# Layer 1's second convolution as a two-phase filter along the columns: five plane products in place of six, its input's sum on VectorE in two parts

## The chip, the cores and the metric

The kernel runs on one core of a Trainium2 chip. The metric is the device time of one execution in microseconds (us); lower is better. TensorE (PE) multiplies matrices, VectorE (DVE) and ScalarE (ACT) work on elements, GpSimd (POOL) works on elements and issues DMAs, SyncE (SP) issues DMAs.

## The reference, cut to what matters

x has 16 images of 16 channels of 256 x 256 in fp32. Layer 0 is a Fourier-type layer that the change doesn't touch. Layer 1 computes, with H = 128:

```
f     = mish(conv2d(each channel alone, W1 (4,1,3,3)))        # 4 features for each channel
top, bot = f[:, :, :128], f[:, :, 128:]
ker   = Wspan * relu(Wred . bot)                              # 9 taps for each position
top_inv = sum over the 3x3 taps of patches(top) * ker         # "involution"
shuffled = rows of top_inv, then of bot rolled by one channel # 64 planes of 256 x 256
out   = mish(conv2d(shuffled, W2 (16,64,3,3)) + b2)           # the second convolution
gate  = sigmoid(3-tap filter over channels of mean(out))
result = x * gate (added to the layer's input)
```

Of `out` only the mean of each channel over all positions is used.

## The kernel before, in words

Layer 0 takes the first 3,500 us or so. Layer 1 (function `layer1`) cuts each image b into nine units, s = 0 to 8: eight full ones and a smaller tail unit. A unit runs through

- `lower` (L1042): first convolution of the lower half, two groups of matmuls through `conv1` (L1029) into the two-buffer PSUM pool `ps1`, four Mish activations on ACT (L1048, `bot`);
- `reduce` (L1050): `pr` matmuls with 32 output columns (L1056), two Relu (L1065, `r`);
- `upper(0)` and `upper(1)` (L1068): first convolution of the upper half, each one group in `ps1` (L1029) and eight Mish activations of 32 partitions (L1077, `wide`); the tail unit has `upper(0)` alone;
- `spread` (L1084): eight copies on POOL (L1089, L1090);
- `involution(0)` to `involution(3)` (L1092): each two groups of a `pd` matmul (L1097) and three VectorE operations (L1105, L1108), then stores of the result to `cf` in DRAM by POOL's DMAs (L1119 to L1131); `bot` is stored too (L1149).

The second convolution works an image later. `conv2_rows` (L1154) loads `rows`, 17 pairs of image rows with 64 planes each, into one of two SBUF buffers `rows2`. In a partition, `rows` holds per pair 258 values: a zero, the 128 odd columns, the 128 even columns, a zero. So the even columns and the odd columns are two planes, and one 3-tap filter along the columns is three products of a shifted plane with a weight. `conv2(b, s, acc)` (L1159) is a generator with two parts, q = 0 for the odd output columns and q = 1 for the even ones. Each part makes three plane products (dx) times two blocks of rows (blk) times four 32-column tiles of PE (j) into one PSUM tile `c2ps`, and a Mish on ACT (L1182) whose accumulator adds up the output. The pool `ps2` of `c2ps` has one buffer. An fp32 matmul leaves two records in the trace: a product is 8 matmuls of the program, 16 records; a part has 48 records.

PE, ACT, DVE and POOL run in the order in which the program is written (a manual schedule); each engine goes through its own list in order and waits at semaphores. DMAs on SP are placed by a scheduler. In step i, with `now` unit i, `nxt` unit i + 1 and `second` the convolution of the image before, the order is (L1256 to L1295):

```
begin_unit(i + 2); conv2_rows for the next step; second = conv2(b - 1, s, acc)
nxt.lower(); now.involution(0); next(second)     # part q = 0
nxt.reduce(); now.involution(1); nxt.upper(0); now.involution(2)
nxt.upper(1); nxt.spread(); next(second)         # part q = 1
now.involution(3)
```

`begin_unit` loads `z` by SP for two units ahead. In the steps with s = 8 there is no convolution; `gate` (L1185) starts there, in front of `nxt.lower()`: it adds up `acc` on VectorE (`total`, `totals`), multiplies on PE (`pg`, L1205), takes an Exp on ACT, and in the steps that follow scales the image on POOL (L1221) and stores it (L1230). After the last image, eight steps hold the convolution alone: this is called the tail.

Of the kernel before, what the change touches and what calls it, by code (L numbers as in the profile page):

```python
# [10 lines left out]
F32 = mybir.dt.float32  # L11
I32 = mybir.dt.int32
AF = mybir.ActivationFunctionType
ALU = mybir.AluOpType
# [7 lines left out]
P = 128  # L22
# [34 lines left out]
def load(nc, pool, src, shape, name):  # L57
    t = pool.tile(shape, F32, tag=name, name=name)
    nc.sync.dma_start(out=t, in_=src)
    return t  # L60
# [872 lines left out]
def layer1(ctx, tc, d, zn, cf, mr, nb):  # L933
# [7 lines left out]
    nc = tc.nc  # L941
    H = N // 2
    wp = ctx.enter_context(tc.tile_pool(name="l1w", bufs=1))
    zp = ctx.enter_context(tc.tile_pool(name="l1z", bufs=4))
    fp = ctx.enter_context(tc.tile_pool(name="l1f", bufs=2))
    rp = ctx.enter_context(tc.tile_pool(name="l1r", bufs=3))
# [3 lines left out]
    psd = ctx.enter_context(tc.tile_pool(name="psd", bufs=3, space=PSUM))  # L950
    ps2 = ctx.enter_context(tc.tile_pool(name="ps2", bufs=1, space=PSUM))
# [6 lines left out]
    wr = load(nc, wp, d["wr"], [P, 32], "wr")  # L958
    dw = load(nc, wp, d["dw"], [P, P], "dw")
    dwt = load(nc, wp, d["dwt"], [P, P], "dwt")  # L960
    c2 = load(nc, wp, d["c2"], [P, 2, 3, 32], "c2")
    pm = load(nc, wp, d["pm"], [P, 3, C], "pm")
    weca = wp.tile([P, 3], F32, name="weca")
    nc.sync.dma_start(out=weca, in_=d["weca"].to_broadcast([P, 3]))
# [8 lines left out]
    b2 = load(nc, wp, d["b2"], [P, 1], "b2")  # L973
# [20 lines left out]
    for t in rows2:  # L994
        for x in (0, N + 1):
            nc.gpsimd.memset(t[:, :, x : x + 1], 0.0)

    def load_rows(b, half, j, h):

        z = zp.tile([P, 8, N + 2], F32, tag="z", name="z")  # L1000
        flat = z.rearrange("p c x -> p (c x)")
        row = C * (N + 2)
        if j < 4:

            m = 8 * (N + 2) - 2
            src = zn[b, H * half + 30 * j, 8 * h, 0:1]
            for dx in range(3):
                win = bass.AP(src.tensor, src.offset + dx, [[row, 32], [1, m]])
                nc.sync.dma_start(out=flat[32 * dx : 32 * dx + 32, :m], in_=win)
            for i in range(2):  # L1010
                win = bass.AP(src.tensor, src.offset + (32 + i) * row, [[1, 3], [1, m]])
                nc.sync.dma_start(out=flat[96 + 3 * i : 99 + 3 * i, :m], in_=win)
            return z
        m = 4 * (N + 2) - 2
        src = zn[b, H * half + 120, 0, 0:1]
        for dx in range(3):
            for c in range(4):
                p = 40 * dx + 10 * c
                win = bass.AP(src.tensor, src.offset + dx + 4 * (N + 2) * c, [[row, 10], [1, m]])
                nc.sync.dma_start(out=flat[p : p + 10, :m], in_=win)  # L1020
        return z
# [132 lines left out]
    def conv2_rows(b, s):  # L1154
        t = rows2[(8 * b + s) % 2]
        flat = cf[b % 4].rearrange("(t y) f c x -> (y f c) t x", y=2)
        nc.sync.dma_start(out=t[:, :, 1 : N + 1], in_=flat[:, 16 * s : 16 * s + 17])

    def conv2(b, s, acc):  # L1159


        t = rows2[(8 * b + s) % 2]

        begin = ((H + 1, 1, H + 2), (0, H + 1, 1))
        for q in range(2):

            pool, tag = (psd, "d") if q and b == nb - 1 else (ps2, "c2")
            ps = pool.tile([P, 4, H], F32, tag=tag, name="c2ps")
            for blk in range(2):
                for dx in range(3):  # L1170
                    x = begin[q][dx]
                    for j in range(4):
                        nc.tensor.matmul(  # L1173
                            ps[32 * j : 32 * j + 32],
                            lhsT=c2[:, blk, dx, :],
                            rhs=t[:, 4 * j + blk : 4 * j + blk + 4, x : x + H],
                            start=(blk, dx) == (0, 0),
                            stop=(blk, dx) == (1, 2),
                        )
            e = rp.tile([P, 4, H], F32, tag="e2", name="e2", bufs=2)  # L1180
            k = 2 * s + q
            nc.scalar.activation(e, ps, AF.Mish, bias=b2, accum_out=acc[:, k : k + 1])  # L1182
            yield

    def gate(b, acc):  # L1185

# [53 lines left out]
    def begin_unit(i):  # L1240
        if i < len(order):
            b, s = order[i]
            units[i] = Unit(b, i, *blocks[s])

    E = mybir.EngineType
    with tc.manual_schedule(engines={E.PE, E.Activation, E.DVE, E.Pool}):
        begin_unit(0)
        begin_unit(1)
        u = units[0]
        u.lower()  # L1250
        u.reduce()
        u.upper(0)
        u.upper(1)
        u.spread()
        acc, last = None, iter(())
        for i in range(9 * nb + 12):  # L1256
            b, s = divmod(i, 9)
            now, nxt = units.pop(i, None), units.get(i + 1)
            begin_unit(i + 2)
            second = iter(())  # L1260
            if s == 8 and b < nb:
                conv2_rows(b, 0)
            if s == 8 and b and b <= nb:
                last = gate(b - 1, acc)
                next(last)
            if s < 8 and b and b <= nb:
                if s == 0:
                    acc = sm.tile([P, 16], F32, tag="acc", name="acc")
                if s < 7:
                    conv2_rows(b - 1, s + 1)  # L1270
                second = conv2(b - 1, s, acc)
            if nxt:
                nxt.lower()
            if now:
                now.involution(0)
            next(second, None)
            if nxt:
                nxt.reduce()
            if s == 8:
                next(last, None)  # L1280
            if now:
                now.involution(1)
            if nxt:
                nxt.upper(0)
            if now:
                now.involution(2)
            if s == 8:
                next(last, None)
            if nxt:
                nxt.upper(1)  # L1290
                nxt.spread()
            next(last, None)
            next(second, None)
            if now:
                now.involution(3)  # L1295
# [159 lines left out]
@with_exitstack  # L1455
def forward(ctx, tc, d):
    nb = d["x"].shape[0]
    dram = ctx.enter_context(tc.tile_pool(name="dram", bufs=1, space=DRAM))
    keep = ctx.enter_context(tc.tile_pool(name="keep", bufs=1))
    al = dram.tile([NF, 2, 64, nb, N], F32, name="al")  # L1460
    bd = dram.tile([nb, P, P], F32, name="bd")
    hd = dram.tile([2, 2, 64, nb, C, N], F32, name="hd")
    tabs = (
        dram.tile([P, 2, C, N], F32, name="td"),
        dram.tile([NF, P, 384], F32, name="avd"),
        dram.tile([P, 2, C, N], F32, name="ed"),
    )
    zn = dram.tile([nb, N + 2, C, N + 2], F32, name="zn")
    cf = dram.tile([4, N + 2, 4, C, N], F32, name="cf")
    mr = keep.tile([P, nb, G, 2], F32, name="mr")  # L1470
    layer0_forward(tc, d, al, bd, tabs)
    layer0_mix(tc, d, al, hd, tabs)
    layer0_back(tc, d, hd, bd, zn, mr, tabs[2])
    layer1(tc, d, zn, cf, mr, nb)
# [25 lines left out]
```

## Time and profile before

| what | value |
|---|---|
| three runs, median (lowest to highest) | 7309.22 us (7302.86 to 7325.03) |
| the profiled execution: its own time, its span | 7312.28 us, 7310.5 us |
| mean granted PE clock | 0.969 |
| busy share of the span: PE, DVE, ACT, POOL | 92%, 68%, 52%, 47% |
| L1173, PE, the second convolution | 12288 records, 1391.9 us busy |
| L1182, ACT, its Mish | 256 of 687 ns |
| L1077, ACT, Mish of `upper` | 2176 of 680 ns |
| L1108, L1105, DVE, involution | 2176 of 691 ns, 1088 of 684 ns |

The time is that of one execution; the span is from the first to the last instruction of the profile, and the rest lies around it. Busy shares are averages over stages with different limits: a share below 100% doesn't say that an engine has room in every stage. PE's records overlap: the duration of one is longer than its distance to the next.

### The profile page before, as it was taken

Reading aid. Unit: us, or ns where it says so; the run is one execution under the profiler, and the core shown is the slowest. Engines: PE = TensorE matmul, PEld = TensorE weight load, DVE = VectorE, ACT = ScalarE, POOL = GpSimd, SP = SyncE. Lnnn points to the kernel's source line nnn. Section 1 sums busy time; section 2 is a strip of 40 time slices with the busy share of each in tenths; the row PEclk is TensorE's granted clock in tenths of the full one; section 3 lists DMA queues with packets and bytes.
Section 4 is the critical chain, followed back from the end, with each engine's and each line's share of the span. In section 5 each row is a group of like instructions: output and inputs, shape, how many; then the busy total and the mean of one; then the engine's idle time right before and its main releaser. Section 6 shows DMA issues by size and latency. Waiting matters only on the chain.

```text
span 7310.5 us, 147410 instructions
## 1 busy us (share of the span) xinstructions
PE 6750.3 (92%) x57640; PEld 3787.1 (52%) x57640; DVE 4970.2 (68%) x9465; ACT 3811.4 (52%) x5915; POOL 3470.0 (47%) x4612
## 2 busy tenths in 40 slices
PE   7889999899999998999789999999999999999997
PEld 5777778666667776777433333333333333333332
DVE  8999975466666665888666666666666666666662
ACT  2223333466666665222366666666666666666662
POOL 2334445322222222666554666556665555655663
PEclk9889999999999999999899999999999999999998
DMA  3344444433333333999767888888888888888886
GB/s 100 112 115 125 119 125 125 124 100 97 96 94 98 99 99 107 321 327 326 227 195 218 249 256 257 249 259 248 267 260 243 253 248 268 253 247 254 252 267 219
DMA packets 716089, 1443.59 MB, mean 197 GB/s; under 512 B 98954, under 2 KB 525254, under 8 KB 673638
## 3 DMA queue, kind: packets, MB, share of 16 engines
q1 hardware_dynamic: 567206, 959.76, 43.8%
q0 software_dynamic: 148192, 474.40, 20.9%
q8 instruction: 460, 7.54, 0.4%
q14 instruction: 231, 1.89, 0.1%
HBM read 877.12 MB, written 556.47 MB: 196 GB/s over the span
## 4 chain that ended last, share of the span: by engine, by line
PE 71%; DVE 16%; DMA 4%; ACT 4%; issue 3%; POOL 1%; SPq 0%; DVEq 0%; ACTq 0%; POOLq 0%
PE c2ps L1173 18%; PE c L1029 12%; PE pd L1097 12%; PE ph L700 5%; PE ps L643 5%; PE pg L665 4%; PE px L313 3%; ACT wide L1077 3%; DVE alb L607 2%; PE pu L207 2%; PE pr L1056 2%; PE py L860 2%; PE pv L214 2%; PE py L861 2%; DVE u L224 2%
## 5 line engine op out<-in xcount | busy, mean ns | idle before, releaser
L1077 ACT ACTIVATE wide<-c,b 32x512 f32<-32x512 f32 x2176 | 1479.3, 680 | 354.2 <-PE c L1029 302.6
L1105 DVE TENSOR_TENSOR t<-pd,r 64x512 f32<-64x512 f32 x1088 | 744.3, 684 | 1287.8 <-PE pd L1097 1262.3
L1108 DVE TENSOR_TENSOR top<-pd,t 32x512 f32<-32x512 f32 x2176 | 1504.1, 691 | 53.7 <-DMA cf<-bot 1.2
L1173 PE MATMUL c2ps<-rows,c 128*32 128x512 f32 x12288 | 1391.9, 600 | 16.4 <-DMA rows<-cf 16.4
L1089 POOL COPY wide<-wide 32x1031 f32<-32x1031 f32 (+1 forms) x576 | 569.6, 989 | 1236.2 <-ACT wide L1077 1208.7
L1029 PE MATMUL c<-z,w 102*128 102x512 f32 x2048 | 1014.5, 628 | 139.2 <-ACT wide L1077 116.6
L1097 PE MATMUL pd<-wide,dw 128*128 128x512 f32 x2048 | 1013.1, 617 | 6.0 <-ACT r L1065 2.9
L1173 PEld LDWEIGHTS c2ps<-rows,c 128*32 128x32 f32 x12288 | 400.3, 109 | 972.0 <-issue 891.6
L720 POOL DMA_DIRECT2D hd<-h x512 | 324.3, 640 | 1198.7 <-DVE h L713 1174.1
L1029 PEld LDWEIGHTS c<-z,w 102*128 102x128 f32 x2048 | 401.5, 198 | 676.5 <-issue 486.9
L1097 PEld LDWEIGHTS pd<-wide,dw 128*128 128x128 f32 x2048 | 377.1, 194 | 613.6 <-issue 447.5
L1182 ACT ACTIVATE e<-c2ps,b 128x512 f32<-128x512 f32 x256 | 176.0, 687 | 831.1 <-PE c2ps L1173 828.4
L1090 POOL COPY wide<-wide 32x1031 f32<-32x1031 f32 (+1 forms) x576 | 573.0, 995 | 36.1
L700 PE MATMUL ph<-ix,yt 64*128 64x256 f32 x4128 | 502.3, 390 | 7.2 <-issue 6.6
L643 PE MATMUL ps<-tt,lt 128*64 128x256 f32 x4224 | 495.5, 384 | 12.6 <-DMA tt<-td 10.0
L313 PE MATMUL px<-wxn,u 128*64 128x256 f32 x4224 | 481.9, 379 | 8.0 <-ACT o L320 7.9
L207 PE MATMUL pu<-fy,eo 128*128 128x128 f32 x2048 | 426.8, 292 | 26.8 <-DVE u L224 21.8
L700 PEld LDWEIGHTS ph<-ix,yt 64*128 64x128 f32 x4128 | 393.1, 190 | 94.0 <-issue 46.8
L1048 ACT ACTIVATE bot<-c,b 128x512 f32<-128x512 f32 x544 | 344.3, 684 | 175.2 <-PE c L1029 167.9
L873 POOL TENSOR_TENSOR x<-x,o 128x512 f32<-128x512 f32 x256 | 324.4, 1267 | 216.6 <-DVE o L872 198.5
L607 DVE TENSOR_SCALAR alb<-alc,m 128x1024 f32<-128x1024 f32 x330 | 419.9, 1396 | 0.0
L214 PE MATMUL pv<-at,eo 128*128 128x128 f32 x2048 | 413.3, 285 | 0.0
(204 smaller groups left out, 10418.6 us busy)
## 6 DMA issues: line engine op xcount, KB each, us to landing
rows<-cf SPq DMA_DIRECT2D x128, 2176.0 KB
z<-zn SPq DMA_DIRECT2D x768, 257.8 KB
cf<-top POOLq DMA_DIRECT2D x512, 240.0 KB, 7.0
cf<-bot POOLq DMA_DIRECT2D x96, 840.0 KB, 11.6
alc<-al SPq DMA_DIRECT2D x264, 256.0 KB
zn<-zb SPq DMA_DIRECT2D x128, 516.0 KB
o<-zn SPq DMA_DIRECT2D x128, 516.0 KB
z<-in_x SPq DMA_DIRECT2D x64, 1024.0 KB
```

Of the source, the lines that this page charges most:

```text
L207: nc.tensor.matmul(pu[:, xh, e].rearrange("p v m -> p (v m)"), lhsT=lhs, rhs=fy[:, e], start=True, stop=True,)
L313: nc.tensor.matmul(ps[64 * k : 64 * k + 64, :, h], lhsT=u[:, h, part, g0 + j + k].rearrange("p f c -> p (f c)"), rhs=wxn[:, h, part], star ...
L643: nc.tensor.matmul(ps[64 * h : 64 * h + 64, v], lhsT=lt[:, h, k, 1 - v : 3 - v].rearrange("p l f c -> p (l f c)"), rhs=tt[:, h, k], start= ...
L700: nc.tensor.matmul(ph[q][:, e], lhsT=yt[lanes, i].rearrange("p t k -> p (t k)"), rhs=ix[lanes, i], start=n == 0, stop=n == 3,)
L1029: nc.tensor.matmul(ps[:, a], lhsT=w, rhs=z[:k, c : c + 2, 0:N], start=True, stop=True)
L1077: nc.scalar.activation(self.feat[64 - 32 * q : 96 - 32 * q, f, self.groups[g], :H], ps[q][32 * f : 32 * f + 32], AF.Mish, bias=b1[0][32 * ...
L1089: nc.gpsimd.tensor_copy(flat[0:32, f, 1:m], flat[64:96, f, 0 : m - 1])
L1090: nc.gpsimd.tensor_copy(flat[96:128, f, 0 : m - 1], flat[32:64, f, 1:m])
L1097: nc.tensor.matmul(ps, lhsT=dwt if self.tail else dw, rhs=self.feat[:, f, cs, :H], start=True, stop=True,)
L1105: nc.vector.tensor_tensor(t[64:128], ps[:64], self.r[:, cs], ALU.mult)
L1108: nc.vector.tensor_tensor(self.top[32 * f : 32 * f + 32, cs, q], ps[lanes], t[lanes], ALU.add)
L1173: nc.tensor.matmul(ps[32 * j : 32 * j + 32], lhsT=c2[:, blk, dx, :], rhs=t[:, 4 * j + blk : 4 * j + blk + 4, x : x + H], start=(blk, dx) = ...
```

## The change

With the odd column plane O, the even column plane E and the weights w0, w1, w2 of the three taps, the kernel before computes even(k) = w0 O(k-1) + w1 E(k) + w2 O(k) and odd(k) = w0 E(k) + w1 O(k) + w2 E(k+1): six products. The changed kernel computes A(k) = w1 E(k) (one product, copied from PSUM to SBUF by ACT into `mid`), even(k) = A(k) + w0 O(k-1) + w2 O(k) (two products), pair(k) = E(k) + O(k-1) (a sum on VectorE of two SBUF inputs, rows 0 to 8 and then rows 9 to 16), and odd(k) = w0 pair(k) + (w1 + w2) pair(k+1) - [w0 O(k-1) + w2 O(k) + A(k+1)] (two products and a subtraction). The weights w1 + w2 are added up once (`c2s`). VectorE takes `even`, `both` and `odd` out of PSUM; the Mishes read SBUF. `conv2` now has four parts, placed at other points of the step: A after `involution(0)`, the two products of `even` after `involution(1)`, those of `odd` in front of `involution(3)`, and the Mish of `odd` after the next step's `lower`. `conv2_rows` stands in front of `lower` as before, and `gate` now starts after `lower`. In the last image the products of `even` take a buffer of the pool `psd`, as part q = 1 did.

```diff
+    c2s = wp.tile([P, 2, 32], F32, name="c2s")
+    nc.vector.tensor_tensor(c2s, c2[:, :, 1], c2[:, :, 2], ALU.add)
...
+    pair = wp.tile([P, 17, H + 1], F32, name="pair")
+    mid = [wp.tile([P, 4, H + 1], F32, name=f"mid{i}") for i in range(2)]
+    for t in mid:
+        nc.gpsimd.memset(t[:, :, H : H + 1], 0.0)
...
     def conv2(b, s, acc):
         t = rows2[(8 * b + s) % 2]
-        begin = ((H + 1, 1, H + 2), (0, H + 1, 1))
-        for q in range(2):
-            pool, tag = (psd, "d") if q and b == nb - 1 else (ps2, "c2")
+        def sums(lo, hi):
+            nc.vector.tensor_tensor(
+                pair[:, lo:hi], t[:, lo:hi, H + 1 :], t[:, lo:hi, : H + 1], ALU.add
+            )
+
+        def products(terms, n=0):
+            pool, tag = (psd, "d") if n % 2 and b == nb - 1 else (ps2, "c2")
             ps = pool.tile([P, 4, H], F32, tag=tag, name="c2ps")
-            for blk in range(2):
-                for dx in range(3):
-                    x = begin[q][dx]
+            for i, (w, src, x) in enumerate(terms):
+                for blk in range(2):
                     for j in range(4):
                         nc.tensor.matmul(
                             ps[32 * j : 32 * j + 32],
-                            lhsT=c2[:, blk, dx, :],
-                            rhs=t[:, 4 * j + blk : 4 * j + blk + 4, x : x + H],
-                            start=(blk, dx) == (0, 0),
-                            stop=(blk, dx) == (1, 2),
+                            lhsT=w[:, blk],
+                            rhs=src[:, 4 * j + blk : 4 * j + blk + 4, x : x + H],
+                            start=(i, blk) == (0, 0),
+                            stop=(i, blk) == (len(terms) - 1, 1),
                         )
-            e = rp.tile([P, 4, H], F32, tag="e2", name="e2", bufs=2)
+            return ps
+
+        def pooled(y, q):
             k = 2 * s + q
-            nc.scalar.activation(e, ps, AF.Mish, bias=b2, accum_out=acc[:, k : k + 1])
-            yield
+            nc.scalar.activation(y, y, AF.Mish, bias=b2, accum_out=acc[:, k : k + 1])
+
+        a = mid[s % 2]
+        nc.scalar.copy(a[:, :, :H], products([(c2[:, :, 1], t, H + 1)]))
+        sums(0, 9)
+        yield
+        ps = products([(c2[:, :, 0], t, 0), (c2[:, :, 2], t, 1)], 1)
+        even = rp.tile([P, 4, H], F32, tag="even", name="even", bufs=2)
+        nc.vector.tensor_tensor(even, ps, a[:, :, :H], ALU.add)
+        both = rp.tile([P, 4, H], F32, tag="both", name="both", bufs=2)
+        nc.vector.tensor_tensor(both, ps, a[:, :, 1:], ALU.add)
+        sums(9, 17)
+        yield
+        pooled(even, 0)
+        ps = products([(c2[:, :, 0], pair, 0), (c2s, pair, 1)])
+        odd = rp.tile([P, 4, H], F32, tag="odd", name="odd", bufs=2)
+        nc.vector.tensor_tensor(odd, ps, both, ALU.subtract)
+        yield
+        pooled(odd, 1)
+        yield
...
-        acc, last = None, iter(())
+        acc, last, second = None, iter(()), iter(())
         for i in range(9 * nb + 12):
...
-            second = iter(())
             if s == 8 and b < nb:
                 conv2_rows(b, 0)
+            if s < 7 and b and b <= nb:
+                conv2_rows(b - 1, s + 1)
+            if nxt:
+                nxt.lower()
+            next(second, None)
+            second = iter(())
             if s == 8 and b and b <= nb:
                 last = gate(b - 1, acc)
                 next(last)
             if s < 8 and b and b <= nb:
                 if s == 0:
                     acc = sm.tile([P, 16], F32, tag="acc", name="acc")
-                if s < 7:
-                    conv2_rows(b - 1, s + 1)
                 second = conv2(b - 1, s, acc)
-            if nxt:
-                nxt.lower()
             if now:
                 now.involution(0)
             next(second, None)
...
             if now:
                 now.involution(1)
+            next(second, None)
             if nxt:
                 nxt.upper(0)
```

## The prediction

> **What bounds the kernel now.** I read the page first: busy shares, then the chain that ended last.
>
> ```profile
> PE 6750.3 (92%) x57640; PEld 3787.1 (52%) x57640; DVE 4970.2 (68%) x9465; ACT 3811.4 (52%) x5915; POOL 3470.0 (47%) x4612
> ```
>
> ```profile
> PE 71%; DVE 16%; DMA 4%; ACT 4%; issue 3%; POOL 1%; SPq 0%; DVEq 0%; ACTq 0%; POOLq 0%
> PE c2ps L1173 18%; PE c L1029 12%; PE pd L1097 12%; PE ph L700 5%; PE ps L643 5%; PE pg L665 4%; PE px L313 3%; ACT wide L1077 3%; DVE alb L607 2%; PE pu L207 2%; PE pr L1056 2%; PE py L860 2%; PE pv L214 2%; PE py L861 2%; DVE u L224 2%
> ```
>
> TensorE carries the chain, and the convolution that changes (L1173) is its largest line. It is not clear from this what a shorter L1173 is worth, so I went to layer 1 alone, first by stage (busy us of PE, PEld, DVE, ACT, POOL, then clock, DMA share), then one step in order of time.
>
> ```profile
> 5000.00:5500.00 500.00, 484.61 (x2476) 174.42 (x2469) 311.75 (x462) 309.94 (x490) 295.26 (x410) 0.98 0.87 261
> ```
>
> ```profile
> 5019.13 1.88 PE L1029 MATMUL c<-z,w 102*128 102x512 f32 x4
> 5020.85 1.88 PE L1097 MATMUL pd<-wide,dw 128*128 128x512 f32 x4
> 5022.57 1.88 PE L1029 MATMUL c<-z,w 102*128 102x512 f32 x4
> 5024.38 5.43 PE L1173 MATMUL c2ps<-rows,c 128*32 128x512 f32 x48
> 5029.74 1.98 PE L1097 MATMUL pd<-wide,dw 128*128 128x512 f32 x4
> 5031.56 3.60 PE L1029 MATMUL c<-z,w 102*128 102x512 f32 x8
> 5035.00 1.88 PE L1097 MATMUL pd<-wide,dw 128*128 128x512 f32 x4
> ```
>
> ```profile
> 5021.11 11.27 ACT L1077 ACTIVATE wide<-c,b 32x512 f32<-32x512 f32 x16 [2.19 <-PE c L1029]
> 5032.40 0.69 ACT L1182 ACTIVATE e<-c2ps,b 128x512 f32<-128x512 f32 x1
> ```
>
> See that PE has no idle time, and how near ScalarE is. The 16 Mishes L1077 end at 5032.38. The second half of the next `lower` (PE, at 5031.56 + 1.72 = 5033.28) needs the PSUM buffer that the last Mish frees. PE is only 0.84 late of it. From start to start a full step is pr 1.01, pd 1.82, c 1.72, pd 1.72, c 1.81, c2ps 5.36, pd 1.82, c 3.44, pd 1.81, c2ps 5.22: 25.73 us.
>
> A batch is six such steps, one of 24.0, one of 17.9 and one of about 29.5; 15 batches run so, and the last one's convolution runs alone at the end.
>
> **What the Trainium skill says.** (1) "VectorE: DVE Perf Modes", section on the TRN2 errata: an fp32 `tensor_tensor` takes (N+151)/0.96 ns; for 512 elements 691 ns. The trace agrees: L1108 691, L629 676 (two SBUF inputs). (2) "GPSIMD Engine Reference", Key points: GpSimd shares SBUF interfaces with VectorE and contends with DVE instructions that have two SBUF inputs. No row of this trace isolates that. (3) "TensorE: Matmul & The Clock Gate", Why this matters: idle gaps over some 3 us drop the PE clock. The trace agrees: of the PE gaps beside the clock records 27 of 28 near 3.5 us are followed by a drop, 2 of 65 near 1.5 us, none of 32 near 1 us. At each batch's boundary it looks so (4 records take 3.78, not 1.88):
>
> ```profile
> 4922.83 3.78 PE L1029 MATMUL c<-z,w 102*128 102x512 f32 x4 [3.60 <-ACT wide L1077]
> 4928.47 3.77 PE L1029 MATMUL c<-z,w 102*128 102x512 f32 x4 [1.86 <-ACT wide L1077]
> ```
>
> **The change, part by part.**
> *PE.* Per block 96 records become 80. One record is 5.22/48 = 0.109, so -1.74 us. But the products now stand in three places, not two: A (16 records) before `pr`, P2 (32) before `upper(0)`, P3 (32) before `involution(3)`. Going to 32-column tiles and back costs 0.09 + 0.14 + 0.10 = 0.33 (1.81, 5.36 and 1.82 against 1.72, 5.22 and 1.72). PE's own step is 25.73 - 1.74 + 0.33 = 24.32.
>
> *The ScalarE loop.* Between the two groups of Mishes PE must run second `lower` group, involution(0), A, `pr`, involution(1), P2, `upper(0)`. From `upper(0)`'s start: 1.98 to the first Mish, 11.27 of Mishes, 0.06 to PE, then 1.72 + 1.81 + 1.74 + 1.01 + (1.82 + 0.09) + (3.48 + 0.14) + 0.10 = 25.22. The same loop before is 13.31 + 1.72 + 1.81 + 5.22 + 1.01 + 1.82 = 24.89, hidden under 25.73. A and P2 are as long as the old first half: all that is saved lies outside this loop. So the step becomes 25.22, -0.51, and PE idles 0.90 at the second `lower` group: that wait is what is late next.
>
> The step that ends on the tail unit (8 Mishes, not 16) has no such loop: there the full -1.41 stays. At the boundary PE waits for ScalarE anyway (3.60 + 1.86 above): 0. A batch: 6 x -0.51 - 1.41 = -4.5; 15 of them -67.
>
> *VectorE.* Added per block: `even`, `both`, `odd` 3 x 0.69, sums of 9 x 129 = 1161 and 8 x 129 = 1032 elements at 1.37 and 1.23 by the skill's formula: 4.7. Busy goes from 16.5 (a 26 us window) to 21.2 of 25.2. Cover: from involution(0)'s start VectorE is done with involution(1) at 1.16 + 4.3 + 1.37 + 4.3 = 11.1, P2 ends on PE at 10.1; `even`, `both` and the second sum (2.6) end 3.7 after P2, P3 starts 5.4 after P2. Hidden with 1.7 to spare, and P3 is outside the ScalarE loop, so PE's 0.90 of idle time covers as much again. Bounds for the sums: 2.6 (formula) to 5.2 (each doubled by GpSimd). The sum below takes 2.6; doubled would still be nearly hidden in full steps and cost the boundary some 2 to 3 us a batch, up to 45. Below nothing is excluded: no VectorE work is removed.
>
> *ScalarE.* One copy (586 ns, L672's row) more per block, and its Mishes read SBUF, 0.69 as before. `pooled(odd)` and the copy stand behind `lower`'s four Mishes, before `r`; the copy must end before P2, 2.9 of PE work later. Hidden; without cover 0.6 a step. The gate's `total` now waits for a `pooled(odd)` behind those Mishes, some 2 us later in the boundary step, where `pg` holds PE: 0 to 1 us a batch, value 0.2 (3 us).
>
> *SP and POOL.* `rows` are free earlier (after P2 and the second sum); the load is still issued behind the same z loads, at the same place. Bytes and issues are the same; in 25.2 instead of 25.7 us the DMA share of 0.87 becomes 0.89 (0.92 to 0.94 in the steps that also carry the gate's traffic, where before five rows loads came 0.7 to 1.4 late). I take +8, ends 0 and +25. The memsets and c2s are once: under 3.
>
> *The tail.* Eight blocks alone, now bound partly by rows:
>
> ```profile
> 7179.37 21.05 PE L1173 MATMUL c2ps<-rows,c 128*32 128x512 f32 x192
> 7206.00 11.93 PE L1173 MATMUL c2ps<-rows,c 128*32 128x512 f32 x96 [5.58 <-DMA rows<-cf]
> 7219.66 21.05 PE L1173 MATMUL c2ps<-rows,c 128*32 128x512 f32 x192 [1.72 <-DMA rows<-cf]
> 7245.29 33.65 PE L1173 MATMUL c2ps<-rows,c 128*32 128x512 f32 x288 [4.58 <-DMA rows<-cf]
> ```
>
> 12.5 a block. After: `odd` and back to PE 1.1, A and P2 5.2, wait for `even`, `both`, second sum 2.6 to 3.0, P3 3.5: 12.4 to 12.8. No gain, and gaps of 2.6 are near what drops the clock (half of six such gaps did): 0 to +25, I take +6.
>
> **Sum.** -67 + 3 + 8 + 6 = -50. The profiled execution took 7312.28 (span 7310.5), 3.1 above the runs' median 7309.2. Against it 7262, as a median about 7259.
>
> **Rivals.**
> *R1, the transfers take it back.* DMA share 0.87 to 0.94 speaks for it, only five late loads in 15 batches against. If every gated step saturates, the gain of four steps (4 x 0.51 x 15 = 31) goes and the tail loses 10: 7290.
> *R2, the full PE gain.* If the Mishes got ahead (the loop is a count of rows, 0.9 over PE's 24.32), every step would save 1.41: 7 x 1.41 x 15 = -148, 7165. The 0.84 of slack speaks against it.
> *R3, slower: VectorE becomes the bound through the sums.* Place: the sums, whose second SBUF input is read against GpSimd's copies and scalings (11 to 20 us busy in a 26 us step). It decides from 25.7 - 16.5 - 2.1 = 7.1 us of sums a step, 2.7 times the formula. At three times, 7.8, the step is 26.4, +0.7 x 105 = +70, and the tail's chain +20: 7400. Against: the first sum falls into GpSimd's DMA issues, the second ahead of its copies.
> *R4, it doesn't do what it says:* the tile switch costs as much as the saved records (it would need 1.7, not 0.33): 7310.
>
> **Chances.** Forecast 0.63 (its own range 7225 to 7287), R1 0.14, R2 0.07, R3 0.10, R4 and other ties 0.06. A measurement tells 0.3% (22 us) from no change. Faster: forecast, R2 and a part of R1, 0.75; same 0.15; slower 0.10. The range leaves out R2 and R3: 7222 to 7305.
>
> **What would show it.** PE of a full step near 25.2 with a wait of 0.9 at L1037's second group for ScalarE; three excursions of 16, 32, 32 records; sums of 1.2 to 1.4; a step of 22.6 where it was 24.0. Wrong would be: P3 waiting on VectorE in full steps, PE without waits at 24.3, or `rows` waits in most batches.

## The result, and the profile after

| kernel | median of its runs (lowest to highest) | ratio to before, 95% interval |
|---|---|---|
| before | 7319.01 us (7302.86 to 7325.76) | |
| changed | 7272.96 us (7255.94 to 7279.26) | 0.9935 (0.992 to 0.995) |

The kernel is faster by 46 us, 0.65%. The profiled execution of the changed kernel has a span of 7271.2 us, 39.3 less than the 7310.5 of before.

The busy shares of the changed kernel, from its page:

```profile
PE 6603.5 (91%) x55592; PEld 3651.8 (50%) x55592; DVE 5587.6 (77%) x10106; ACT 3876.9 (53%) x6043; POOL 3524.5 (48%) x4614
```

The same stage as shown before (busy us of PE, PEld, DVE, ACT, POOL, then clock, DMA share and GB/s):

```profile
5000.00:5500.00 500.00, 468.89 (x2202) 157.68 (x2202) 399.37 (x557) 322.17 (x513) 299.44 (x407) 0.98 0.87 259
```

PE went from 484.6 to 468.9 busy in 500 us: it has idle time now, 31 us where it had 15. VectorE went from 312 to 399, ScalarE from 310 to 322, and the DMA share stayed at 0.87. So TensorE no longer sets the pace of this stage alone. One full step of the changed kernel on PE, in order of time:

```profile
5023.64 2.08 PE L1105 MATMUL pd<-wide,dw 128*128 128x512 f32 x4
5025.65 3.69 PE L1185 MATMUL c2ps<-rows,c 128*32 128x512 f32 x32
5029.26 1.99 PE L1037 MATMUL c<-z,w 102*128 102x512 f32 x4
5031.08 1.88 PE L1105 MATMUL pd<-wide,dw 128*128 128x512 f32 x4
5032.80 1.88 PE L1037 MATMUL c<-z,w 102*128 102x512 f32 x4
5034.61 1.92 PE L1185 MATMUL c2ps<-pair,c 128*32 128x512 f32 x16
5036.35 1.90 PE L1185 MATMUL c2ps<-pair,c2s 128*32 128x512 f32 x16
5038.18 1.98 PE L1105 MATMUL pd<-wide,dw 128*128 128x512 f32 x4
5040.00 1.88 PE L1037 MATMUL c<-z,w 102*128 102x512 f32 x4
5042.65 1.98 PE L1037 MATMUL c<-z,w 102*128 102x512 f32 x4 [0.76 <-ACT wide L1085]
5044.47 1.88 PE L1105 MATMUL pd<-wide,dw 128*128 128x512 f32 x4
5046.28 1.97 PE L1185 MATMUL c2ps<-rows,c 128*32 128x512 f32 x16
5048.07 1.03 PE L1064 MATMUL pr<-bot,wr 128*32 128x512 f32 x8
5049.03 2.06 PE L1105 MATMUL pd<-wide,dw 128*128 128x512 f32 x4
```

The lines show the three excursions to the 32-column tiles of the convolution, of 32, 32 and 16 records (below: P2, P3 and A, as in the prediction), and the one wait: the second group of `lower` waits 0.76 us for the last Mish of `wide`. From `pd` at 5023.64 to the next at 5049.03 the step is 25.39 us.

PE's waits of over 0.15 us between 3,900 and 7,100 us, from the view of the waits (total us, number, longest):

```profile
PE c L1037 <- ACT wide L1085: 150.5, 114, 3.6
PE c2ps L1185 <- DMA rows<-cf: 19.0, 12, 4.3
```

The first line is the wait above, 86 times in the full steps with some 67 us together; the other 28 waits, 84 us, are those of the boundaries between images. The second line is the one I had put too low: `rows` comes late, in the step s = 3 in 11 of the 14 images of the table below.

The mean length of each step, from the start of its `pr` matmuls to those of the next, over the images 2 to 15 of the profiles (a step s begins in the middle of unit s's work; an empty field means no such wait):

| step s | 0 | 1 | 2 | 3 | 4 | 5 | 6 | 7 | 8 |
|---|---|---|---|---|---|---|---|---|---|
| before | 29.86 | 25.73 | 25.72 | 25.91 | 25.88 | 25.72 | 25.73 | 24.03 | 17.89 |
| changed | 26.60 | 25.33 | 25.42 | 26.87 | 25.50 | 25.38 | 25.40 | 22.63 | 20.80 |
| of it, wait for `rows`: before | | | | 0.19 | 0.13 | | | | |
| of it, wait for `rows`: changed | | | | 1.30 | 0.06 | | | | |

The steps s = 8 and s = 0, the boundary between two images, are to be read as a pair: the change moves products of the convolution from the second into the first.

### The profile page after: what moved, and what is told of

It reads as the page before. It is cut to its first block, busy times and chain, and to the rows that moved or that the text cites. A ratio compares the mean times of both kernels' runs of the same rounds, so it can differ in the third digit from the quotient of the medians.

```text
span 7271.2 us, 144305 instructions
## 1 busy us (share of the span) xinstructions
PE 6603.5 (91%) x55592; PEld 3651.8 (50%) x55592; DVE 5587.6 (77%) x10106; ACT 3876.9 (53%) x6043; POOL 3524.5 (48%) x4614
## 4 chain that ended last, share of the span: by engine, by line
PE 37%; DMA 5%; ACT 4%; DVE 3%; issue 1%; POOL 0%; SPq 0%; DVEq 0%; ACTq 0%; POOLq 0%
PE c2ps L1185 14%; PE c L1037 11%; PE pd L1105 10%; ACT wide L1085 3%; DMA rows<-cf 3%; DVE top L1116 1%; PE pr L1064 1%; DMA z<-zn 1%; DVE t L1113 1%; DMA cf<-bot 0%; SPq L1017 0%; DVE pair L1175 0%; ACT L1085 0%; ACT bot L1056 0%; POOL o L1253 0%
## 5 line engine op out<-in xcount | busy, mean ns | idle before, releaser
L1037 PE MATMUL c<-z,w 102*128 102x512 f32 x2048 | 1046.0, 636 | 212.3 <-ACT wide L1085 190.8
L1037 PEld LDWEIGHTS c<-z,w 102*128 102x128 f32 x2048 | 384.0, 197 | 818.3 <-issue 488.8
L1185 PE MATMUL c2ps<-rows,c 128*32 128x512 f32 x6144 | 722.9, 603 | 24.6 <-DMA rows<-cf 19.0
L207 PE MATMUL pu<-fy,eo 128*128 128x128 f32 x2048 | 427.0, 292 | 26.5 <-DVE u L224 21.8
L1185 PEld LDWEIGHTS c2ps<-rows,c 128*32 128x32 f32 x6144 | 176.7, 109 | 533.5 <-issue 400.3
L651 DVE COPY s<-ps 128x512 f32<-128x512 f32 x264 | 265.7, 1024 | 189.0 <-PE ps L643 171.2
L665 PE MATMUL pg<-alb,s 128*32 128x64 f32 x16896 | 274.1, 221 | 132.3 <-issue 86.4
```

What stands on the lines that cost most here:

```text
L207: nc.tensor.matmul(pu[:, xh, e].rearrange("p v m -> p (v m)"), lhsT=lhs, rhs=fy[:, e], start=True, stop=True,)
L1037: nc.tensor.matmul(ps[:, a], lhsT=w, rhs=z[:k, c : c + 2, 0:N], start=True, stop=True)
L1185: nc.tensor.matmul(ps[32 * j : 32 * j + 32], lhsT=w[:, blk], rhs=src[:, 4 * j + blk : 4 * j + blk + 4, x : x + H], start=(i, blk) == (0, 0 ...
```

## The experiments

The theory: (a) behind PE lies the loop through ScalarE's Mishes, which gives back most of what the filter saves in a full step; (b) behind that loop lies the late load of `rows` in the steps with the gate's traffic. The rivals: VectorE, with 88 us more in 500, sets the step; or the changed order of the main loop, not the filter, makes the difference.

**1. P2 out of ScalarE's loop.**

```diff
             if now:
                 now.involution(1)
-            next(second, None)
             if nxt:
                 nxt.upper(0)
+            next(second, None)
```

> The two products of even (P2) move from in front of upper(0) to behind it, all else as in the changed kernel. Theory (ScalarE's loop of Mishes sets the full step): the loop loses P2's 3.6 us, so PE's own work is the bound; a full step goes from 25.36 to 24.6 (its 25.38 less the 0.77 wait, which disappears), about 0.77 x 6 x 15 = 69 us less where rows are in time; time about 7205 to 7220. Rival, transfers: rows come late in the steps with the gate's traffic instead, four of the six keep their length, gain 25 to 35 us. Rival, VectorE: P3 waits for the second sum, since P2 now ends only two blocks of PE work ahead of it; the step stays over 25.

Measured: 7271.63 us, ratio 0.9935 (0.9923 to 0.9948): no gain over the changed kernel. Both forecasts of the time missed, that of the theory and the 25 to 35 us of the rival. But the steps s = 1, 2, 5 and 6 are 24.42, 24.45, 24.34 and 24.38, and PE's wait for `wide` is gone from them. The step s = 3 has become 30.43 us. PE in one such step, in order of time:

```profile
5211.53 3.60 PE L1037 MATMUL c<-z,w 102*128 102x512 f32 x8
5214.97 1.88 PE L1105 MATMUL pd<-wide,dw 128*128 128x512 f32 x4
5222.24 3.64 PE L1185 MATMUL c2ps<-rows,c 128*32 128x512 f32 x16 [5.39 <-DMA rows<-cf]
```

`lower` runs without a break (8 records in 3.60), and A waits 5.39 us for `rows`; the clock drops after it (16 records in 3.64, not 1.97). Over the image the wait is 4.84 + 0.23 us on average. From the view of the waits:

```profile
PE c2ps L1185 <- DMA rows<-cf: 71.0, 13, 9.6
```

So (a) holds: with the loop loosened a full step whose `rows` are in time falls by 0.9 to 1.0, to PE's own 24.35. The step s = 3 gives 3.56 us of it back, with the wait for `rows`; that (b) is the reason is what experiments 5 to 7 test. Another 0.87 us is lost in s = 8, which went from 20.80 to 21.67: there P3 takes 4.45 us instead of 3.57, because P2 now ends so late that the second sum isn't ready in time. So the rival VectorE was right in that one step. The stage view of this kernel shows the DMA engines full in two windows of gated steps (second number from the end):

```profile
4958.00:4985.00 27.00, 27.00 (x146) 8.97 (x148) 23.94 (x34) 18.84 (x30) 21.30 (x29) 1.00 0.98 286
4985.00:5010.00 25.00, 19.36 (x92) 6.48 (x88) 15.55 (x22) 11.95 (x21) 16.18 (x23) 0.93 1.00 271
```

In the windows that follow, to 5115, the share is 0.76 to 0.95.

**2. The sums twice.**

```diff
         def sums(lo, hi):
-            nc.vector.tensor_tensor(...)
+            for _ in range(2):
+                nc.vector.tensor_tensor(...)
```

> Both sums on VectorE are issued twice (same result), so VectorE has 2.6 us more in every step with a convolution, 3 or more where GpSimd scales the image. Theory (VectorE has cover): full steps stay at 25.4 to 25.6; the boundary step and the tail (2.6 us for each of eight blocks on their chain, or half of it) pay, together +30 to +55 us against the changed kernel, 7300 to 7325. Rival (VectorE is already the bound of the step): +2.6 x 120 = +310 us, about 7580.

Measured: 7369.93 us, ratio 1.007 (1.0056 to 1.0084). Steps s = 1, 2, 5, 6 are 25.29, 25.49, 25.35 and 25.37, as in the changed kernel: 2.6 us more on VectorE cost these full steps nothing (s = 3 and 4 grew by a quarter of a us each). Their effect can be seen all the same: P3 takes 4.3 to 4.7 us in these four steps instead of 3.57, since its later rows need the second sum, and PE's wait for `wide` has gone from 0.76 to under 0.1. P3 lies outside ScalarE's loop, so what it loses only fills the idle time that the loop leaves to PE. This is a second sign of (a). The two boundary steps and s = 7 took 4.2 us an image more (63 us), the tail 29. My price for these, 30 to 55 together, was too low; VectorE as the bound of the full step would have cost 310. It is not the bound in the changed kernel, but in s = 7, 8 and the tail it has no cover left.

**3. The order alone.** The kernel before with its six products:

```diff
-            if s == 8 and b and b <= nb:
-                last = gate(b - 1, acc)
-                next(last)
...
+            if s < 7 and b and b <= nb:
+                conv2_rows(b - 1, s + 1)
             if nxt:
                 nxt.lower()
+            if s == 8 and b and b <= nb:
+                last = gate(b - 1, acc)
+                next(last)
```

> The kernel before with the changed order alone: the load of rows and lower ahead of the convolution's generator, gate behind lower; six products in two parts as before. Theory: the order is worth nothing, within 10 us of the kernel before, full steps 25.73, boundary two steps 47.5 to 47.8. Rival: the gate behind lower is what shortened the two boundary steps (47.7 to 47.4 in the profiles); then this kernel is 5 us faster than before.

Measured: 7319.79 us, ratio 1.0004 (0.9996 to 1.0012); full steps 25.7, the two boundary steps 17.89 + 29.81 = 47.70. The order is worth nothing to six products; so the 46 us are put down to the filter and the places of its parts.

**4. Fewer Mishes.**

```diff
                 for q in range(2):
+                    if (f, q) == (3, 1):
+                        continue
                     nc.scalar.activation(
```

> Leaves out two of the 16 Mish activations of a full unit's upper half (that part of wide keeps its zeros), all else as in the changed kernel: takes 1.41 us out of ScalarE's loop and nothing out of PE, VectorE, GpSimd or the transfers. Theory: the wait of 0.77 at lower's second group disappears, full steps 24.6, about -70 us in them, and the boundary shortens by up to 1.4 x 15 = 21; batch 0 too (8 x 1.4): 7165 to 7190. Rival, transfers: rows waits take most of it, over 7235. Rival, VectorE: the step stays at 25.4, since VectorE isn't relieved; only batch 0 and the boundary gain, 7240.

Measured: 7263.86 us, ratio 0.9919 (0.9904 to 0.9934): the rival of the transfers was right on the time, and the 7165 to 7190 of the theory was wrong. The wait for `wide` left the full steps (s = 5: 24.33, s = 6: 24.39), and s = 3 is 33.09 us, with 6.87 of waiting for `rows`. The step s = 1 stays at 25.56: there PE waits 0.76 on average for GpSimd's copies of `wide`. Shortening ScalarE's side of the loop does what moving PE's work out of it did, and ends at the same place.

**5. The gate's traffic left out**, with P2 behind `upper(0)`:

```diff
         for k in range(0, 8, 2):
+            if b < nb - 1:
+                yield
+                continue
```

> P2 behind upper(0) as in the first experiment, and for all images but the last the gate's loads, its scaling on GpSimd and its stores are left out (those images of the output stay unwritten). Theory (behind ScalarE's loop the transfers of the steps with the gate's traffic are the bound): the rows wait of 4.84 us in the step s = 3 disappears, steps s = 1 to 6 all 24.35; about -(4.84 + 0.23) x 15 = -76 us against the first experiment, about 7195. Since GpSimd no longer scales beside it, the first sum takes 1.37 us everywhere, against a mean of 1.69. Rival (the load of rows is late of its own, by its place behind the z loads): the wait stays over 2 us, 7240 or more.

Measured: 7170.94 us, ratio 0.9793 (0.9779 to 0.9806), 101 us below experiment 1. Steps s = 2 to 6 are all 24.35 to 24.37, s = 1 is 24.27, and no wait for `rows` is left in them. The gain is more than the 76 I expected from the waits: the step s = 3 of experiment 1 is 25.59 even without its wait of 4.84, so 1.24 more than 24.35, which is 19 us in 15 images. That fits the slowed clock behind the wait, as in experiment 1's lines. The first sum's row, from the groups by shape:

```profile
L1175 DVE TENSOR_TENSOR pair<-rows 128x1161 f32<-128x1161 f32 x128 | 175.4, 1370 | 3.7
```

In the changed kernel the same group is

```profile
L1175 DVE TENSOR_TENSOR pair<-rows 128x1161 f32<-128x1161 f32 x128 | 216.8, 1693 | 4.4 <-DMA rows<-cf 0.7
```

**6. rows ahead of z**, with P2 behind `upper(0)`:

```diff
+            if s < 7 and b and b <= nb:
+                conv2_rows(b - 1, s + 1)
             begin_unit(i + 2)
             if s == 8 and b < nb:
                 conv2_rows(b, 0)
-            if s < 7 and b and b <= nb:
-                conv2_rows(b - 1, s + 1)
```

> P2 behind upper(0), and the load of rows is issued ahead of the z loads of the unit after next instead of behind them. Bytes the same. Theory (DMA engines are full over five gated steps): the backlog only moves from rows to z; the sum of waits for transfers in these steps stays within a third of 5.1 us a batch, 7245 to 7275. Rival (order on SP's queue): rows are in time, all six steps 24.35, 7195.

Measured: 7178.11 us, ratio 0.9803 (0.979 to 0.9816). Here my theory was wrong and the rival right: the same bytes, in another order on SP's queue, and the waits for `rows` are gone but for one:

```profile
PE c2ps L1185 <- DMA rows<-cf: 2.1, 1, 2.1
PE c L1037 <- DMA z<-zn: 4.1, 2, 2.9
```

On SP's queue the load of `rows` stood behind ten z loads. In experiment 1, where PE could start on this `rows` only at 4999.15, after 5.64 us of waiting:

```profile
4960.59 6.99 SPq L1017 DMA_DIRECT2D z<-zn  x3
4967.62 0.68 SPq L1020 DMA_DIRECT2D z<-zn  x2
4968.41 4.62 SPq L1017 DMA_DIRECT2D z<-zn  x3
4973.65 1.26 SPq L1020 DMA_DIRECT2D z<-zn  x2
4975.76 0.39 SPq L1165 DMA_DIRECT2D rows<-cf  x1
```

From the issue of `rows` for s = 3 to its first use, the wait included, there were 21.8 us on average in the changed kernel and 22.6 in experiment 1; now there are 33.5. The issue itself comes 26.9 us after that of the step before, no longer 36.9. Full DMA engines make the load slow, but it is late because it is issued behind ten z loads. The z loads, which are for a unit two steps away, can nearly stand the delay: they cost two waits, 4.1 us in all. GpSimd scales the image here as before; so it was not its scaling, which experiment 5 left out too, that held the step up.

**7. The gate's traffic over eight steps**, with P2 behind `upper(0)`, `rows` behind z as before:

```diff
-            following = [part(k + 2), part(k + 3)] if k < 6 else None
+            following = []
             for half, o in enumerate(parts):
+                if k < 6:
+                    following.append(part(k + 2 + half))
...
+                if half == 0 and b < nb - 1:
+                    yield
```

> P2 behind upper(0), and the gate's loads, scalings and stores of an image go over eight steps (one half image quarter each) instead of four; the same work and bytes. Theory: DMA share falls below full in the first four steps, no rows waits over 1 us a batch, steps 24.35, time 7195 to 7215. Rival (the mean demand is already too high, 0.91 of the DMA engines at this pace): the waits of some 5 us a batch come two or three steps later, 7250 to 7270.

Measured: 7169.41 us, ratio 0.9789 (0.9773 to 0.9805): full steps 24.28 to 24.38, no wait for `rows`. The time is 26 us under the forecast of 7195 at the least, which counted the waits alone, as in experiment 5. So either remedy is enough: fewer bytes in the first four steps, or an earlier issue.

**8. P2 behind `upper(0)`, rows first, spread, and the second sum ahead of `even`.** The last part:

```diff
         ps = products([(c2[:, :, 0], t, 0), (c2[:, :, 2], t, 1)], 1)
+        sums(9, 17)
...
-        sums(9, 17)
```

> P2 behind upper(0), rows ahead of z, the gate's traffic over eight steps, and the second sum issued ahead of even and both instead of behind them. Theory: as the spread alone, and P3 no longer waits 1.8 to 2.1 us for the second sum in the tail's eight blocks: -8 to -14 us more; 7185 to 7205. Rival (rows then bind the tail, as in the kernel before): the tail gains under 5 us.

Measured: 7139.75 us (7136.31 to 7141.44), ratio 0.9749 (0.9736 to 0.9763): the fastest of all, 2.5% below the kernel before, and 45 us under the forecast, which built on the too high one of experiment 7 and on 8 to 14 us for the second sum. A block of the changed kernel's tail, on PE:

```profile
7202.82 5.44 PE L1185 MATMUL c2ps<-rows,c 128*32 128x512 f32 x48 [0.79 <-DVE odd L1212]
7208.04 1.06 PE L1185 MATMUL c2ps<-pair,c 128*32 128x512 f32 x4
7210.89 1.48 PE L1185 MATMUL c2ps<-pair,c 128*32 128x512 f32 x10 [1.78 <-DVE pair L1175]
```

and of this one's:

```profile
7078.65 5.42 PE L1185 MATMUL c2ps<-rows,c 128*32 128x512 f32 x48 [0.80 <-DVE odd L1212]
7083.87 1.92 PE L1185 MATMUL c2ps<-pair,c 128*32 128x512 f32 x16
7085.58 1.92 PE L1185 MATMUL c2ps<-pair,c2s 128*32 128x512 f32 x16
```

P3 no longer waits for the second sum; a block takes 9.7 us instead of 12.5, and from the `pr` of the last full unit to the end there are 165.0 us, against 180.9 in experiment 7. In the boundary step s = 8 P3 takes 3.57 us again, and the step is 20.80 (in experiment 7: 4.33 and 21.54). The new place of the second sum was not run alone; but with `rows` first (experiment 6) or the spread (7) P3 still lost this time. A `rows` wait of 4.10 us is left in the tail.

**9. rows first alone**, in the changed kernel (the edit of experiment 6, with P2 in its place):

> The changed kernel with one edit: the load of rows is issued ahead of the z loads; P2 stays in front of upper(0). Theory (ScalarE's loop sets the full steps, and the late rows in s = 3 are a cost apart): the rows wait of 1.30 us a batch goes, s = 3 becomes 25.4 as the others, the full steps keep their 25.3 to 25.4 and their wait of 0.77; -20 us, about 7253 on the scale of 7273. Rival (late rows cause part of the long steps elsewhere): the other full steps fall below 25.3 too, -40 us or more.

Measured: 7257.13 us, ratio 0.9917 (0.9899 to 0.9934). The step s = 3 is 25.41, and steps 1 to 6 all keep their wait of 0.76 to 0.84 for `wide`, so the two costs are apart. The time is 16 us below that of the changed kernel, but the two intervals overlap, and the sum hides two terms: the steps of an image are 1.8 us shorter together, and the tail is 3.9 us longer.

**10. Six products, gate spread** (the edit of experiment 7 in the kernel before):

> The kernel before (six products, its own order) with the gate's traffic over eight steps. Theory: PE alone sets its full steps, so only its few late rows (0.32 us a batch) and nothing else can go: full steps 25.73, within 10 us of the kernel before; the gain of the last experiments over it is then the filter's, at its new places. Rival (the spread traffic itself is worth something to any kernel): 30 us or more faster than before.

Measured: 7306.65 us, ratio 0.9986 (0.9979 to 0.9992), 12 us below before; full steps 25.71 to 25.74. That is 2 us over my limit of 10, and far from the rival's 30. So the spread helps the two-phase filter, which needs it, and hardly the six products.

## Why the prediction was right, point by point

The forecast was -50 us; measured were -46 in the medians and -39 in the spans of the two profiles. The mechanism was right: the loop through ScalarE's Mishes, and not PE's saving, sets the full step. That the total came so near is in part luck, for several terms were off and their errors cancel.

- **PE's own step.** 24.32 was worked out from 16 records less and one excursion more. With both other bounds away (experiments 5, 7, 8) it is 24.35. R4 is refuted.
- **ScalarE's loop.** The wait stands where it was put, at `lower`'s second group, 0.76 to 0.84 instead of 0.90. The loop was taken as 25.22 and is 25.39. From the lines above: the second `lower` group after its wait takes 1.82, not 1.72, and the `pd` in front of P2 1.99 to 2.01, not 1.91; the rest of the loop agrees within 0.02. So a full step saved 0.3 to 0.4, in s = 3 less, and not 0.51. Over six steps and 15 images that is some 28 us, where 46 were forecast.
- **The tail unit's step.** Predicted -1.41, measured 24.03 to 22.63, -1.40: 21 us, as forecast.
- **The boundary.** Taken as 0 and +0.2 an image; the two steps went from 47.75 to 47.40. In 15 images this is -5 us, where +3 was forecast. The 3.60 us wait stayed, and `pg` has a new wait (0.25), as foreseen. That the order alone gives no such gain is shown by experiment 3; why PE's saving comes through here in part was not tested.
- **SP and the transfers.** This term was mis-sized: +8, ends 0 and +25. The waits for `rows` grew from 0.32 to 1.36 us an image, some 15 us in all. "`rows` waits in most batches" was to be a sign of being wrong, and in s = 3 they stand in 11 of 14 images. I had the place (steps with the gate's traffic) and the end of the range, and took too low a value, because I read the DMA share as room and not the time from issue to use: 22.8 us in the kernel before for s = 3, with loads already late (four by the view of the waits, not five).
- **VectorE.** The second sum took 1.23 and the first 1.37, as the formula of the Trainium skill's "VectorE: DVE Perf Modes", section on the TRN2 errata, gave. The prediction had the first sum fall into GpSimd's DMA issues; in s = 2 and 3 it mostly falls beside GpSimd's scaling of the image and took up to 2.95. The upper bound, each sum doubled, was about right for one sum of two, in two steps. The sums cost full steps nothing: even issued twice they cost next to nothing there (experiment 2), so R3 falls for the changed kernel.
- **The tail.** +6 taken for the eight blocks alone. From the first of their products to the last there are 99.6 us before and 101.4 after, +2; the wait for the second sum is 1.77 to 2.08 a block, and one of the eight runs at a slow clock. From the last `pr` to the end there are +6 (153.5 to 159.6), but 3 of these are products that the change moved from s = 0 into s = 8.
- **R1** was half right for this kernel (some 15 us of 31, and nothing in the tail) and nearly wholly right for the next step: where the loop is loosened, the transfers take most of the gain. **R2**, the full gain, needs both bounds away.

In all, from the two profiles: -28 in the full steps without the waits for `rows`, -21 in the tail unit's, -5 at the boundaries, +14 for the waits, +3 in the tail, and -2.5 ahead of the first step with a convolution: -39. The full steps gave 18 us less than forecast and `rows` took 6 more; the boundaries gave 8 back, the tail 3. The start of layer 1's second image moved by up to 12 us between profiled executions of the same layer 0 and first image, so a few us of a single span are not to be explained.

## What to carry to other kernels

When work is taken from the engine that bounds a step, draw the loops that pass through the next engine, and ask on which of them the removed work lay: here five sixths of the products stayed on TensorE, but what remained inside ScalarE's loop was as long as before. The same products, moved out of that loop by one position, gave 1.0 us a step. A step can then run into the next bound at once, as here into a late load: for a load, look at when it is issued and behind what, and not at the share of the DMA engines alone; a queue's order can cost what looks like bandwidth.

## What the runs showed of the hardware that I had not expected

In these traces GpSimd's scalings and the sum, a VectorE operation with two SBUF inputs, slow each other. The step in the changed kernel, first VectorE's lines, then GpSimd's of the same time:

```profile
4967.41 1.39 DVE L1116 TENSOR_TENSOR top<-pd,t 32x512 f32<-32x512 f32 x2
4970.97 2.93 DVE L1175 TENSOR_TENSOR pair<-rows 128x1161 f32<-128x1161 f32 x1
```

```profile
4967.64 2.21 POOL L1253 TENSOR_SCALAR o<-o,scale,mean 128x258 f32<-128x258 f32 x4
4971.03 3.30 POOL L1253 TENSOR_SCALAR o<-o,scale,mean 128x258 f32<-128x258 f32 x4
```

Four scalings take 2.21 us without the sum and 3.30 beside it; the sum takes 1.37 alone and 2.93 beside the scalings. The single records behind the second GpSimd line look like taking turns and not like sharing: the first three scalings take 0.56 us each, as without the sum, and only the fourth takes 1.66; the sum is longer by 1.56, nearly three scalings. Where a sum met only one scaling that started during it, it often took 1.37 to 1.40, and the scaling up to 1.74. No experiment isolates this. By steps the first sum's means are 1.40, 1.48, 2.48 and 2.70 for s = 0 to 3, and 1.37 for s = 4 to 7. The Trainium skill's "GPSIMD Engine Reference" names this contention in its Key points without a size; the VectorE operations beside the scalings that read PSUM and one SBUF input, as `top` at 4967.41, kept their 0.68 to 0.70 each.

A long wait for `rows` also costs the clock: after 5.39 us of idle time the next 16 records took 3.64 us instead of 1.97. That fits experiment 5's gain of 101 us where the waits were 76: of the 25 between, 19 lie in the step s = 3, outside the wait itself. How much of them is the clock was not measured by itself.
